# Three graph layers' neighbour mixes as quarter-array products, with tighter buffers and eight groups under way

## The chip, the cores and the metric

The kernel runs on one core of one Trainium2 chip, with the other cores idle. The metric is the time of the program on the device in microseconds (us), from its first to its last instruction; lower is better. All data are float32. The engines that appear below are TensorE (PE in the profile: matrix products, with its weight loads as PEld), VectorE (DVE), ScalarE (ACT), GpSimd (POOL) and the DMA queue that SyncE (SP) issues to. TensorE writes its results to PSUM, which this kernel uses as eight banks of 128 partitions by 512 float32 columns; the other engines copy them from there to SBUF.

## The reference, cut to what matters

The input is 128 graphs of 64 nodes with 256 features each; all graphs share one 64 x 64 adjacency matrix. Four residual layers follow one another:

```python
h = maximum(layernorm(x), 0); x = x + L0(h, adj, ...)   # two adjacency mixes, then four small LSTMs
h = maximum(layernorm(x), 0); x = x + L1(h, adj, ...)   # Laplacian mix, attention with 4 heads, MLP
h = maximum(layernorm(x), 0); x = x + L2(h, adj, ...)   # graph attention
h = maximum(layernorm(x), 0); x = x + L3(h, adj, ...)   # mixes with eigenvectors U of the Laplacian

# what the change touches:
# L1:  xp  = einsum('mn,bnf->bmf', L_norm, h)           # 64 x 64 mix of the nodes of each graph
# L2:  h_prime = einsum('bij,bjo->bio', attention, Wh)  # a mix of its own for each graph
# L3:  agg = einsum('mn,bnd->bmd', U.T, h)
#      out = relu(agg @ W1 + b1) @ W2 + b2
#      result = einsum('nm,bmd->bnd', U, out)
```

Each mix multiplies a 64 x 64 matrix with the 64 nodes of one graph.

## The kernel before

A tile of 128 partitions holds two graphs of 64 nodes. `X[g]` holds eight tiles (16 graphs); layer 0 works on these eight groups. Layers 1 to 3 work on 16 half groups of `HT = 4` tiles (eight graphs each). Since two graphs lie on the 128 partitions, the 64 x 64 mixing matrices are stored as 128 x 128 block-diagonal matrices: the upper left and the lower right quarter hold the matrix, the other two quarters are zero (`adjTb`, `lapb`, `Ub`, `UTb`, and in layer 2 the transposed attention weights `pT`).

The mixes of layers 1, 2 and 3 go through one helper. For each half of the features (`c`) and each tile (`t`) it multiplies a full 128 x 128 block of the activations (the stationary operand) with the 128 x 128 block-diagonal matrix (the moving operand); the result comes out transposed, features on the partitions:

```python
tok = lambda t: slice(t * P, (t + 1) * P)      # P = 128
bat = lambda b: slice(b * N, (b + 1) * N)      # N = 64

def mix_fm(h, m):
    dst = fm()                                  # a "big" buffer, seen as [128, 2, 512]
    for c in range(2):
        ps = bank("mix")
        for t in range(HT):
            PE.matmul(ps[:, tok(t)], h[:, t, tok(c)], m(t), start=True, stop=True)
        evac(dst[:, c, :], ps, 1)               # ScalarE copy of 128 x 512
    return dst

# layer 1:  lx = mix_fm(h, lambda t: lapb)
# layer 2:  aT = mix_fm(h, lambda t: pT[:, tok(t)])
# layer 3:  aT = mix_fm(h, lambda t: Ub)
# ... and layer 3's second mix, on 128 hidden features:
ps = bank("u")
for t in range(HT):
    PE.matmul(ps[:, tok(t)], hid[:, t, :], UTb, start=True, stop=True)
V.tensor_tensor(uT, ps.rearrange("p (t f) -> p t f", t=HT), vec(C3), op=ALU.add)
```

Layer 1's attention already uses 64 x 64 products, in two runs of 32 products per half group. Each product takes one quarter of the array: which half of the partitions its operands lie on picks the rows, which half of the partitions the result goes to picks the columns.

```python
ps = [bank("qk") for m in range(2)]
half = lambda i: slice(i * N, i * N + N)
with plan.burst():
    for b, m, r in [(b, m, r) for b in range(2 * HT) for m in range(2) for r in range(2)]:
        PE.matmul(ps[m][half(r ^ m), bat(b)], qT[half(r), m, bat(b)], kT[half(r), m, bat(b)], start=True, stop=True)
...                                              # softmax, transposes
po = [bank("o") for i in range(2)]
with plan.burst():
    for m, t, i, r in [(m, t, i, r) for m in range(2) for t in range(HT) for i in range(2) for r in range(2)]:
        PE.matmul(po[i][half(r), bat(m * HT + t)], v[half(i), t, bat(2 * m + r)], pT[half(i), m, bat(2 * t + (r ^ m))], start=True, stop=True)
```

The order of instructions on each engine is not that of the source. All operations are recorded first; then a list scheduler on the host (`Plan`) walks through a cost model and fixes each engine's order, the buffer that each value gets and the bank that each product writes. `plan.burst()` makes a run of products one operation of that plan. The parts that matter here:

```python
def burst(self):
    ...
    self.run.cost = 0.3 + 0.036 * len(self.run.calls)    # us, in the plan's model

def rank(self, op):
    ...                                                  # lower goes first
    g = min(max(op.group, 0), self.ends)
    return (g, 8 * max(op.group - g, 0) - op.path, op.index)

# pools
"big": [C([P, HT * (D + 2)], f"big{i}") for i in range(NBIG)],     # 8 buffers of 1032 columns
...
def more(ap, groups):                  # regions that become "big" buffers once `groups` are done
    n = HT * (D + 2)
    for i in range(ap.shape[1] // n):
        late["big", len(pools["big"])] = groups
        pools["big"].append(ap[:, i * n:(i + 1) * n])

more(arena[:, (NG - NEARLY) * GT * D:], (EIG,))          # 6144 columns
more(whh[3], tuple(range(NG)))                           # 2048 columns
more(mids, tuple(range(NG)))                             # 4096 columns
...                                                      # later: each of six X places, 2048 columns

def window(oldest):                    # how many groups may be under way
    return max(oldest, 0) + 2 - oldest if oldest < NG - 1 else max(oldest, REST) + 6 - oldest
```

So after layer 0 at most six half groups are under way at once. The eigenvectors of layer 3 are computed beside layer 0, mostly on VectorE.

Of the kernel before, what the change touches and what calls it, by code (L numbers as in the profile page):

```python
# [8 lines left out]
ALU = mybir.AluOpType  # L9
# [3 lines left out]
N = 64  # L13
# [53 lines left out]
class Plan:  # L67
# [34 lines left out]
    @contextmanager  # L102
    def burst(self):

        self.run, self.whole = None, True
        yield
        self.run.cost = 0.3 + 0.036 * len(self.run.calls)
        self.run.lat = self.run.cost + 0.22
        self.run, self.whole = None, False

# [206 lines left out]
    def rank(self, op):  # L317
        if op.group == self.aside:
            return (-2 if op.eng == "PE" else 1000, op.index)
        if op.eng == "SP":  # L320
            return (op.group, 0, op.index)
        g = min(max(op.group, 0), self.ends)
        return (g, 8 * max(op.group - g, 0) - op.path, op.index)

    def issue(self):
        real = lambda a: a.real() if isinstance(a, Virt) else a
# [538 lines left out]
P = 128  # L865
D = 256
NT = 64
GT = 8
NG = NT // GT
HT = 4  # L870
# [3 lines left out]
SETUP, WEIGHTS, ATTN, REST, EIG = -1, NG, NG + 1, NG + 2, 1000  # L874
NBIG, NMID, NSTAT, NATTN = 8, 8, 14, 4
# [36 lines left out]
def gnn_kernel(ctx: ExitStack, tc: tile.TileContext, a, out):  # L912
    nc = tc.nc
# [3 lines left out]
    def C(shape, name):  # L917
        return pool.tile(list(shape), F32, name=name)
# [4 lines left out]
    whh = [None] + [C([P, 8 * D], f"Whh{p}") for p in range(1, 4)]  # L923
    mids = C([P, NMID * 512], "mids")
    pools = {
        "big": [C([P, HT * (D + 2)], f"big{i}") for i in range(NBIG)],
        "mid": [mids[:, i * 512:(i + 1) * 512] for i in range(NMID)],
        "stat": [C([P, HT * 10], f"stat{i}") for i in range(NSTAT)],
        "attn": [wih[3][:, i * HT * P:(i + 1) * HT * P] for i in range(NATTN)],
# [3 lines left out]

    def more(ap, groups):

        n = HT * (D + 2)
        for i in range(ap.shape[1] // n):
            late["big", len(pools["big"])] = groups
            pools["big"].append(ap[:, i * n:(i + 1) * n])
# [3 lines left out]
    more(mids, tuple(range(NG)))  # L943

    def window(oldest):
        return max(oldest, 0) + 2 - oldest if oldest < NG - 1 else max(oldest, REST) + 6 - oldest

    def reserve(kind, oldest):
        if oldest < NG:
# [8 lines left out]
    plan = Plan(tc, {"PE": nc.tensor, "V": nc.vector, "ACT": nc.scalar, "G": nc.gpsimd, "SP": nc.sync}, pools, late, reserve, window, EIG, REST + NT // HT - 6, slack)  # L958
    PE, V, ACT, G, SP = (plan.proxy(e) for e in ("PE", "V", "ACT", "G", "SP"))

    def bank(name):
        return plan.value("bank")
# [158 lines left out]
    vec = lambda v, n=HT: v.unsqueeze(1).to_broadcast([P, n, v.shape[-1]])  # L1121
    tok = lambda t: slice(t * P, (t + 1) * P)
    bat = lambda b: slice(b * N, (b + 1) * N)

    def tm(n=HT, f=D):

# [173 lines left out]
    def evac(dst, src, i):  # L1300
        if i % 2:
            ACT.copy(dst, src)
        else:
            V.tensor_copy(dst, src)
# [43 lines left out]
    def mix_fm(h, m):  # L1348

        dst = fm()  # L1350
        for c in range(2):
            ps = bank("mix")
            for t in range(HT):
                PE.matmul(ps[:, tok(t)], h[:, t, tok(c)], m(t), start=True, stop=True)
            evac(dst[:, c, :], ps, 1)
        return dst

    def layer1(x):
        h = relu_norm(x)
        lx = mix_fm(h, lambda t: lapb)  # L1360
        x1 = tm()
        for t0 in (0, 2):
            ps = proj_tm(lambda c, t: lx[:, c, tok(t)], Wc, 2, t0)
            V.tensor_add(x1[:, t0:t0 + 2, :], ps.rearrange("p (t f) -> p t f", t=2), vec(bc, 2))
        norm(x1)
        for t0 in (0, 2):
            xp, hp = x1[:, t0:t0 + 2, :], h[:, t0:t0 + 2, :]
            V.tensor_mul(xp, xp, vec(g1, 2))
            G.tensor_add(xp, xp, vec(be1, 2))
            V.scalar_tensor_tensor(xp, xp, 0.0, hp, op0=ALU.max, op1=ALU.add)  # L1370
        x1T = to_fm(x1)
        qT, kT, v = fm(), fm(), tm()
        for m in range(2):
            evac(qT[:, m, :], proj_fm(Wq, x1T, m), 0)
            evac(kT[:, m, :], proj_fm(Wk, x1T, m), 1)
        for t0 in (0, 2):
            evac(pair(v, t0), proj_tm(lambda c, t: x1T[:, c, tok(t)], Wv, 2, t0), 1)
        for t0 in (0, 2):
            G.tensor_add(x1[:, t0:t0 + 2, :], x1[:, t0:t0 + 2, :], vec(bo, 2))


        ps = [bank("qk") for m in range(2)]
        half = lambda i: slice(i * N, i * N + N)
        with plan.burst():
            for b, m, r in [(b, m, r) for b in range(2 * HT) for m in range(2) for r in range(2)]:
                PE.matmul(ps[m][half(r ^ m), bat(b)], qT[half(r), m, bat(b)], kT[half(r), m, bat(b)], start=True, stop=True)
        s = tm(4 * HT, N)
        for m in range(2):
            sm = s[:, m * 2 * HT:(m + 1) * 2 * HT, :]
            V.scalar_tensor_tensor(sm, ps[m].rearrange("p (b k) -> p b k", k=N), 0.125, vec(mask1, 2 * HT), op0=ALU.mult, op1=ALU.add)  # L1390
            stat = plan.value("stat")
            softmax_shift(sm, stat[:, :2 * HT])
            ACT.activation(sm, sm, AF.Exp)
            ssum = stat[:, 2 * HT:4 * HT]
            V.reduce_sum(ssum, sm, axis=AX.X)
            V.reciprocal(ssum, ssum)
            G.tensor_mul(sm, sm, ssum.unsqueeze(2).to_broadcast([P, 2 * HT, N]))

        pT = fm()
        for m in range(2):  # L1400
            evac(pT[:, m, :], transposes([flat(s[:, (m * HT + t) * 2:(m * HT + t) * 2 + 2, :]) for t in range(HT)]), m)
        oT = fm()
# [5 lines that stand above are left out]
        for i in range(2):  # L1408
            evac(oT.rearrange("p c (t b n) -> p c t b n", t=HT, b=2)[:, :, :, i, :], po[i].rearrange("p (c t n) -> p c t n", c=2, t=HT), i)
        x2 = tm()  # L1410
        for t0 in (0, 2):
            ps = proj_tm(lambda c, t: oT[:, c, tok(t)], Wo, 2, t0)
            V.tensor_add(x2[:, t0:t0 + 2, :], ps.rearrange("p (t f) -> p t f", t=2), x1[:, t0:t0 + 2, :])
        norm(x2)
        x2T = fm()
        for c in range(2):
            ACT.activation(x2T[:, c, :], transposes([x2[:, t, tok(c)] for t in range(HT)]), AF.Identity, scale=g2c[:, c:c + 1], bias=be2c[:, c:c + 1])
        V.tensor_mul(x2, x2, vec(g2))
        for t0 in (0, 2):
            G.tensor_add(x2[:, t0:t0 + 2, :], x2[:, t0:t0 + 2, :], vec(b2, 2))  # L1420
        mT = [fm() for i in range(2)]
        for m in range(4):
            ACT.activation(mT[m // 2][:, m % 2, :], proj_fm(W1, x2T, m), AF.Gelu, bias=b1[:, m:m + 1])
        for t0 in (0, 2):
            ps = proj_tm(lambda c, t: mT[c // 2][:, c % 2, tok(t)], W2, 4, t0)
            V.tensor_add(pair(x2, t0), ps, pair(x2, t0))
        for t0 in (0, 2):
            G.tensor_add(x[:, t0:t0 + 2, :], x[:, t0:t0 + 2, :], vec(be3, 2))
        norm(x2)
        for t0 in (0, 2):  # L1430
            V.tensor_mul(x2[:, t0:t0 + 2, :], x2[:, t0:t0 + 2, :], vec(g3, 2))
            V.tensor_add(x[:, t0:t0 + 2, :], x[:, t0:t0 + 2, :], x2[:, t0:t0 + 2, :])

    def layer2(x):
# [16 lines left out]
        V.tensor_max(e, e, e2)  # L1451
        softmax_shift(e, stat[:, :HT])
        attn = plan.value("attn").rearrange("p (t k) -> p t k", t=HT)
        for half in range(2):
            r = slice(half * N, half * N + N)
            ACT.activation(attn[r, :, r], e[r], AF.Exp)
        ssum = stat[:, HT:2 * HT]
        V.reduce_sum(ssum, attn, axis=AX.X)
# [9 lines left out]
    def layer3(x):  # L1468
        h = relu_norm(x)
        for t0 in (0, 2):  # L1470
            G.tensor_add(x[:, t0:t0 + 2, :], x[:, t0:t0 + 2, :], vec(b3b, 2))
        aT = mix_fm(h, lambda t: Ub)
        hid = tm(HT, P)
        ps = bank("hid")
        for t in range(HT):
            for c in range(2):
                PE.matmul(ps[:, tok(t)], aT[:, c, tok(t)], W3a[:, c, :], start=c == 0, stop=c == 1)
        V.tensor_tensor(hid, ps.rearrange("p (t f) -> p t f", t=HT), vec(nb3a), op=ALU.max)
        uT = tm(HT, P)
        ps = bank("u")  # L1480
        for t in range(HT):
            PE.matmul(ps[:, tok(t)], hid[:, t, :], UTb, start=True, stop=True)
        V.tensor_tensor(uT, ps.rearrange("p (t f) -> p t f", t=HT), vec(C3), op=ALU.add)
        for t0 in (0, 2):
            ps = proj_tm(lambda c, t: uT[:, t, :], W3b.unsqueeze(1), 1, t0)
            V.tensor_add(pair(x, t0), ps, pair(x, t0))
# [68 lines left out]
```

## Time and profile before

| | |
|---|---|
| time, median of 3 runs | 2274.92 us (2273.73 to 2276.86) |
| span of the profiled run | 2274.8 us |
| instructions | 33,569 |
| TensorE products (records) | 11,316, busy 2244.4 us |
| VectorE | busy 1685.7 us |
| ScalarE | busy 977.3 us |
| GpSimd | busy 564.0 us |
| last product with `adjTb` (layer 0's mixes) starts at | 1282.9 us |
| first product with `lapb` (layer 1's mix) starts at | 1272.7 us |
| first product with `Ub` (layer 3's mix) starts at | 1547.1 us |

A page of the profile has the busy time of each engine, the span in 40 slices with the busy share of each engine in tenths, and the chain of work that ended last. An engine's group of instructions is named by operation, the result's tile, the operands' tiles, and the shape. Since every instruction passes through the scheduler, all have the same source line (L331), and groups are told apart by tiles and shapes. Each float32 product appears as two records of TensorE (and two weight loads). A record's shape has the moving operand's columns: `128*128 128x256` uses the full array with 256 columns, `64*64 64x64` a quarter with 64 columns. A record's duration includes the way through the array, which overlaps the next record; the interval from one start to the next is what a product costs. "Busy" counts the overlapped stretch once.

### The profile page before, as it was taken

The numbers are of one execution on the slowest core, as the hardware profiler recorded it, in microseconds if no ns is written. First come the engines' busy times: TensorE is split into PE (matmuls) and PEld (weight loads), VectorE is DVE, ScalarE is ACT, GpSimd is POOL, SyncE is SP. The second block draws the span as 40 slices with busy tenths as digits, with TensorE's granted clock in tenths as the row PEclk, the third lists the DMA queues.
The fourth block names the chain that finished last, engine by engine and source line by source line (L and its number), as shares of the span: only waits on it lengthen the run. The fifth ranks groups of instructions, "written<-read, shape, count | busy, mean of one in ns | idle before, by whom it ended". The sixth has DMA issues, their size and how long they took to land.

```text
span 2274.8 us, 33569 instructions
## 1 busy us (share of the span) xinstructions
PE 2244.4 (99%) x11316; PEld 1585.8 (70%) x11316; DVE 1685.7 (74%) x6942; ACT 977.3 (43%) x1915; POOL 564.0 (25%) x856
## 2 busy tenths in 40 slices
PE   9999999999999999999999999999999999999997
PEld 6578468468558558558558658767777677776786
DVE  6656666656799999999988823667678868867775
ACT  3333333333323323323433343455555546555763
POOL 3001100200100100100100203454544655555342
PEclk9999999999999999999999999999999999999999
DMA  7000000000000000000000011000000000000001
GB/s 250 0 1 19 1 1 25 32 1 1 1 1 1 1 1 1 1 1 1 5 1 1 7 38 32 1 1 10 11 20 10 10 29 11 29 10 1 2 18 39
DMA packets 27660, 35.48 MB, mean 16 GB/s; under 512 B 3552, under 2 KB 24928, under 8 KB 26976
## 3 DMA queue, kind: packets, MB, share of 16 engines
q1 hardware_dynamic: 26384, 32.29, 4.2%
q8 instruction: 89, 1.46, 0.3%
q10 hardware_dynamic: 1104, 1.05, 0.2%
q14 instruction: 83, 0.68, 0.1%
HBM read 22.85 MB, written 10.49 MB: 15 GB/s over the span
## 4 chain that ended last, share of the span: by engine, by line
PE 91%; DVE 5%; ACT 2%; POOL 1%; issue 1%; DMA 0%; SPq 0%; DVEq 0%; ACTq 0%
PE bank L331 91%; DVE arena L331 1%; DVE stat L331 1%; DVE big L331 1%; DVE x L331 1%; POOL stat L331 1%; ACT arena L331 1%; DVE mids L331 0%; ACT mids L331 0%; ACT big L331 0%; DMA adj<-in_adj_dram 0%; ACT x L331 0%; ACT Wih L331 0%; DVE Whh L331 0%; POOL x L331 0%
## 5 line engine op out<-in xcount | busy, mean ns | idle before, releaser
L331 PE MATMUL bank<-big,Wih 128*128 128x256 f32 (+2 forms) x2592 | 865.1, 476 | 0.9 <-DVE arena L331 0.3
L331 PEld LDWEIGHTS bank<-big,Wih 128*128 128x128 f32 x2592 | 481.6, 190 | 268.4 <-issue 165.9
L331 ACT ACTIVATE mids<-bank,bl 128x256 f32<-128x256 f32 (+2 forms) x624 | 344.2, 562 | 628.6 <-PE bank L331 617.7
L331 PE MATMUL bank<-big,Whh 128*128 128x256 f32 (+3 forms) x1704 | 538.0, 450 | 0.0
L331 PEld LDWEIGHTS bank<-big,Whh 128*128 128x128 f32 x1704 | 319.3, 191 | 140.3 <-issue 74.6
L331 DVE TENSOR_TENSOR arena<-arena 64x21 f32<-64x21 f32 (+6 forms) x2314 | 374.9, 193 | 34.1 <-POOL arena L331 1.0
L331 POOL TENSOR_SCALAR stat<-stat 128x4 f32<-128x4 f32 (+1 forms) x228 | 66.2, 291 | 726.6 <-DVE stat L331 713.0
L331 DVE TENSOR_TENSOR big<-big,mids 128x256 f32<-128x256 f32 (+2 forms) x192 | 93.7, 488 | 163.5 <-ACT mids L331 162.1
L331 DVE TENSOR_TENSOR big<-mids 128x512 f32<-128x512 f32 (+2 forms) x256 | 145.9, 574 | 37.6 <-ACT mids L331 33.7
L331 ACT ACTIVATE mids<-big 128x256 f32<-128x256 f32 (+2 forms) x176 | 89.8, 510 | 103.5 <-DVE big L331 66.8
L331 DVE TENSOR_SCALAR arena<-arena 64x1 f32<-64x1 f32 (+5 forms) x596 | 117.1, 204 | 8.4
L331 POOL TENSOR_TENSOR stat<-stat,mhalf 128x4 f32<-128x4 f32 (+1 forms) x114 | 119.3, 1049 | 6.8
L331 POOL TENSOR_TENSOR arena<-arena 64x1 f32<-64x1 f32 x66 | 41.9, 635 | 311.5 <-DVE arena L331 165.3
L331 PE MATMUL bank<-Wih,big 128*128 128x256 f32 (+1 forms) x520 | 117.6, 362 | 1.2 <-ACT big L331 1.2
L331 PEld LDWEIGHTS bank<-Wih,big 128*128 128x128 f32 x520 | 90.9, 190 | 20.2 <-issue 8.6
L331 ACT COPY big<-bank 128x512 f32<-128x512 f32 x107 | 59.2, 583 | 80.6 <-PE bank L331 65.4
L331 PEld LDWEIGHTS bank<-adjTb,mids 128*128 128x128 f32 x512 | 70.8, 196 | 26.7 <-issue 17.5
L331 ACT ACTIVATE mids<-x,stat 128x256 f32<-128x256 f32 x92 | 48.6, 592 | 89.7 <-POOL stat L331 89.1
L331 DVE SCALAR_TENSOR_TENSOR arena<-arena 64x1 f32<-64x1 f32 (+4 forms) x389 | 77.2, 205 | 10.5 <-POOL arena L331 4.1
L331 POOL MEMSET arena<- 64x2 f32 (+5 forms) x72 | 8.0, 113 | 309.2 <-DVE arena L331 309.1
L331 DVE BATCH_NORM_STATS2 stat<-x 128x6 f32<-128x256 f32 x228 | 83.4, 409 | 0.0
L331 PE MATMUL bank<-adjTb,mids 128*128 128x128 f32 x512 | 73.6, 282 | 3.0 <-ACT mids L331 2.9
(342 smaller groups left out, 3388.6 us busy)
## 6 DMA issues: line engine op xcount, KB each, us to landing
x<-in_x_dram SPq DMA_DIRECT2D x7, 1024.0 KB, 13.7
out_dram<-x SPq DMA_DIRECT2D x24, 256.0 KB, 2.3
Wih<-in_WihT_dram SPq DMA_DIRECT2D x3, 1024.0 KB, 16.6
Whh<-in_WhhT_dram SPq DMA_DIRECT2D x3, 1024.0 KB, 12.3
put<-x SPq DMA_DIRECT2D x2, 1024.0 KB, 4.6
arena<-put SPq DMA_DIRECT2D x2, 1024.0 KB, 5.0
out_dram<-arena SPq DMA_DIRECT2D x8, 256.0 KB, 2.2
Whh<-in_W_dram SPq DMA_DIRECT2D x2, 512.0 KB, 3.7
```

The source lines that it names most:

```text
L331: getattr(self.engines[op.eng], name)(*map(real, args), **{k: real(a) for k, a in kw.items()})
```

## The change

The mixes of layers 1 to 3 become runs of 64 x 64 products that leave the zero quarters out. A new helper `mix` makes them: per tile and half of the features four products, one for each quarter of the array, where `i` is the graph of the tile and `r` the half of the features. Results of graph `i` go to bank `ps[i]`, so each run writes two banks, and the copies then put the columns of the two graphs back into alternating places of 64. The second mix of layer 3 runs in the same way with 16 products, and its addition of `C3` becomes two of half size. Layer 0's mixes stay as they were.

Beside this, the buffers shrink from 1032 to 1024 columns, so that the regions that are cut into buffers give more of them; the window goes from six to eight half groups; the plan's model of a run's cost goes from 0.3 + 0.036 n to 0.1 + 0.034 n us; and the weight by which later groups stand back goes from 8 to 6.

```diff
-        self.run.cost = 0.3 + 0.036 * len(self.run.calls)
+        self.run.cost = 0.1 + 0.034 * len(self.run.calls)
...
-        return (g, 8 * max(op.group - g, 0) - op.path, op.index)
+        return (g, 6 * max(op.group - g, 0) - op.path, op.index)
...
-        "big": [C([P, HT * (D + 2)], f"big{i}") for i in range(NBIG)],
+        "big": [C([P, HT * D], f"big{i}") for i in range(NBIG)],
...
-        n = HT * (D + 2)
+        n = HT * D
...
-        return ... else max(oldest, REST) + 6 - oldest
+        return ... else max(oldest, REST) + 8 - oldest
...
+    def mix(src, m, nt, nc=2):
+        ps = [bank("mix") for i in range(2)]
+        with plan.burst():
+            for c in range(nc):
+                for t in range(nt):
+                    for i, r in ((0, 0), (0, 1), (1, 0), (1, 1)):
+                        PE.matmul(ps[i][half(r), bat(c * nt + t)], src(t, c)[half(i), half(r)], m(t)[half(i), half(i)], start=True, stop=True)
+        return [p[:, :nc * nt * N].rearrange("p (c t n) -> p c t n", c=nc, t=nt) for p in ps]
...
     def mix_fm(h, m):
         dst = fm()
-        for c in range(2):
-            ps = bank("mix")
-            for t in range(HT):
-                PE.matmul(ps[:, tok(t)], h[:, t, tok(c)], m(t), start=True, stop=True)
-            evac(dst[:, c, :], ps, 1)
+        for i, ps in enumerate(mix(lambda t, c: h[:, t, tok(c)], m, HT)):
+            evac(dst.rearrange("p c (t b n) -> p c t b n", t=HT, b=2)[:, :, :, i, :], ps, 1)
         return dst
...
         uT = tm(HT, P)
-        ps = bank("u")
-        for t in range(HT):
-            PE.matmul(ps[:, tok(t)], hid[:, t, :], UTb, start=True, stop=True)
-        V.tensor_tensor(uT, ps.rearrange("p (t f) -> p t f", t=HT), vec(C3), op=ALU.add)
+        for i, ps in enumerate(mix(lambda t, c: hid[:, t, :], lambda t: UTb, HT, 1)):
+            V.tensor_tensor(uT.rearrange("p t (b n) -> p t b n", b=2)[:, :, i, :], ps[:, 0], vec(C3[:, half(i)]), op=ALU.add)
```

More of the change, by code (lines that the diff above doesn't have):

```diff
@@ L945, in window @@
     def window(oldest):
-        return max(oldest, 0) + 2 - oldest if oldest < NG - 1 else max(oldest, REST) + 6 - oldest
+        return max(oldest, 0) + 2 - oldest if oldest < NG - 1 else max(oldest, REST) + 8 - oldest
     def reserve(kind, oldest):
@@ L1123, in gnn_kernel @@
     bat = lambda b: slice(b * N, (b + 1) * N)
+    half = lambda i: slice(i * N, i * N + N)
+    def mix(src, m, nt, nc=2):
[6 more added lines that the diff above has]
+        return [p[:, :nc * nt * N].rearrange("p (c t n) -> p c t n", c=nc, t=nt) for p in ps]
     def tm(n=HT, f=D):
@@ L1382, in layer1 @@
         ps = [bank("qk") for m in range(2)]
-        half = lambda i: slice(i * N, i * N + N)
         with plan.burst():
@@ L1453, in layer2 @@
         attn = plan.value("attn").rearrange("p (t k) -> p t k", t=HT)
-        for half in range(2):
-            r = slice(half * N, half * N + N)
+        for i in range(2):
+            r = half(i)
             ACT.activation(attn[r, :, r], e[r], AF.Exp)
```

## The prediction

> **What bounds the kernel now.** I read the page's first two parts and its chain first, to find the engine that sets the end.
>
> ```profile
> span 2274.8 us, 33569 instructions
> PE 2244.4 (99%) x11316; PEld 1585.8 (70%) x11316; DVE 1685.7 (74%) x6942; ACT 977.3 (43%) x1915; POOL 564.0 (25%) x856
> ...
> PE   9999999999999999999999999999999999999997
> ...
> DVE  6656666656799999999988823667678868867775
> ...
> PE 91%; DVE 5%; ACT 2%; POOL 1%; issue 1%; DMA 0%; SPq 0%; DVEq 0%; ACTq 0%
> ```
>
> TensorE is busy in every slice, and 91% of the chain is its own work. VectorE is full only in slices 12 to 21 (some 650 to 1250 us), where it computes eigenvectors beside layer 0. Layers 1 to 3 run from about 1270 us, and there VectorE has a quarter to spare. So a product removed from TensorE in that stage should come out of the time, unless a wait takes its place. How much waiting there is already, the busy times by stretch show (columns: stretch, its length, then busy us and instructions of PE, PEld, DVE, ACT, POOL, the clock, the DMA share and GB/s):
>
> ```profile
> 1500.00:1700.00 200.00, 196.95 (x1408) 150.28 (x1411) 144.00 (x415) 114.97 (x198) 100.27 (x137) 1.00 0.03 9
> 1700.00:1900.00 200.00, 195.03 (x1370) 146.44 (x1362) 150.94 (x408) 109.39 (x193) 99.45 (x134) 1.00 0.05 17
> 1900.00:2100.00 200.00, 198.92 (x1526) 147.94 (x1526) 150.81 (x406) 111.01 (x194) 112.61 (x146) 1.00 0.04 14
> 2100.00:2200.00 100.00, 100.00 (x653) 75.96 (x652) 75.22 (x229) 72.19 (x115) 42.52 (x63) 1.00 0.02 6
> 2200.00:2275.00 75.00, 60.01 (x358) 53.78 (x356) 45.01 (x140) 27.05 (x52) 23.29 (x38) 0.93 0.11 36
> ```
>
> TensorE is idle 3.1 + 5.0 + 1.1 + 0 = 9 us from 1500 to 2200, and 15 us in the last 75, where the groups run out. Short waits hide in "busy", because a record's duration includes its way through the array. Taking each record's start minus the one before, less the usual interval of its shape, I get 20 us of waiting from 1500 to 2200, 18 us after, and 51 us in the whole run.
>
> What a product costs is read from the timeline of TensorE alone (start, duration, group; "x" counts records, two to a product):
>
> ```profile
> 1713.23 3.19 PE L331 MATMUL bank<-Wih,arena 128*128 128x256 f32 x14
> 1716.34 1.16 PE L331 MATMUL bank<-arena,big 64*64 64x64 f32 x64
> 1717.44 0.70 PE L331 MATMUL bank<-mids,same 128*128 128x256 f32 x2
> 1717.97 1.01 PE L331 MATMUL bank<-ident,arena 128*128 128x128 f32 x6
> ...
> 1737.25 4.05 PE L331 MATMUL bank<-Whh,x 128*128 128x256 f32 x18
> 1741.14 0.60 PE L331 MATMUL bank<-ident,big 128*128 128x128 f32 x4
> ...
> 1750.10 1.95 PE L331 MATMUL bank<-lapb,big 128*128 128x128 f32 x16
> 1751.88 1.89 PE L331 MATMUL bank<-Wih,mids 128*128 128x256 f32 x8
> ```
>
> The last two lines are one old mix: 16 records, 1751.88 - 1750.10 = **1.78 us**, so 0.111 us a record and 0.222 a product. The first four lines are a run of 32 quarter products, as the attention of layer 1 already has: 1717.44 - 1716.34 = 1.10 us inside. But its neighbours pay as well. A 256-column record takes (1741.14 - 1737.25) / 18 = 0.216 us. The 14 ahead of the run took 3.11 us instead of 3.02: 0.09 more to get in. The two behind it took 0.53 instead of 0.43: 0.10 more to get out. So a run costs 1.10 + 0.09 + 0.10 = **1.29 us**. I looked at all 32 runs of the trace: those that stand alone have 0.94 us from the first to the last record, 0.15 from there to the next product, about 0.1 ahead and 0.1 behind. Within a run, four records start nearly together, then comes the next four 0.059 us later.
>
> **What the Trainium skill says.** "TensorEngine Tiling (Array Packing)", section Tiling Modes, Key Properties, says that tiles of the array work independently, and that changing the tiling mode drains TensorE. The trace agrees with both: 32 products in 1.10 us instead of 32 x 0.11, and about 0.19 us for getting in and out. The same page, Gotcha 1: PSUM Pressure, says that different row tiles write to different PSUM banks and may not share one at once. That is why the new helper needs two banks even for the 16-product mix, which fills half of each; no run before shows what sharing would do. Its section PSUM Bottleneck says that after tiling the copies out of PSUM may become the bound; here ScalarE and VectorE have 45% and 25% to spare in this stage, so I don't expect it.
>
> **The change part by part.**
>
> (1) Three mixes per half group: each removes 8 products and adds a run of 32. 1.78 - 1.29 = 0.49 us saved. There are 16 half groups, so 48 x 0.49 = **23.5 us**.
>
> (2) Layer 3's second mix: 4 products, 4 x 0.222 = 0.89 us, become a run of 16. Eight rounds of four records fewer take 8 x 0.059 = 0.47 us off the run of 1.29, which leaves 0.82. Saved 0.07 us, 16 x 0.07 = **1 us**. The fixed cost of the mode eats this one.
>
> (3) Runs that happen to lie next to each other pay the way in and out once. The trace has one such pair (128 records at 1483 us). With four more runs per half group there will be some more; I allow 1 us.
>
> (4) ScalarE's copies: still two per mix, but with places of 64 columns. Layer 1's attention has such copies: 0.585 us with places of 64 and 0.585 us without, at the median. Nothing added. VectorE gets 16 additions more: one of 128 x 512 at 0.69 us becomes two of 128 x 256. The 128 x 256 additions between SBUF tiles take 0.41 us, so I estimate 2 x 0.41 - 0.69 = 0.13 us, 2 us in all, in a stage where VectorE has a quarter idle. On the path: nothing.
>
> (5) Latency: before, the first bank of a mix could be copied after 4 products (0.9 us), while the other was filled. Now both banks are done at the end of the run (1.1 us), and the copies stand one behind the other: some 0.3 us more from the mix to the next projection, three times per half group. With eight half groups under way this is covered, except at the end, where it adds about 1 us.
>
> (6) Buffers and window: 1024 columns divide the regions without rest. The arena's 6144 columns give 6 instead of 5, one weight region 2 instead of 1, `mids` 4 instead of 3. With the 8 of their own that is 20 instead of 17 after layer 0, and each of the six places of X gives 2 instead of 1 when it comes free. Six groups had 2.8 each, eight have 2.5, then more. So eight groups can be fed, and when one waits on VectorE or GpSimd another has a product ready. The plan's cost of a run falls from 0.3 + 0.036 x 32 = 1.45 us to 1.19, nearer to the 1.29 measured, so planned and real order fit better. I estimate that the 20 us of waits from 1500 to 2200 fall by some 12, and the 18 us at the end by 2 (a weight of 6 instead of 8 lets the last groups finish closer together), less the 1 us of (5). Together **13 us**. This is a judgement, the other terms are arithmetic.
>
> (7) Layer 0 has none of these mixes, and TensorE waits 6 us in it after 50 us: nothing to gain.
>
> Sum: 23.5 + 1 + 1 + 13 = 38.5 us; 2274.9 - 38.5 = **2236 us**, 1.7% less.
>
> **The rivals.** (A) The products saved turn into waits. If the helpers (VectorE, 75% busy; two banks held by each run; GpSimd's slow steps) set the pace, TensorE idles more and only a few us of 25 remain: about 2262 us. For it: the waits above end on VectorE and ScalarE, and the plan's order is fixed ahead, so a late operation stops all behind it. Against it: no helper is over 76% in any stretch, and 100 us went by at 2100 without idle time. (B) The schedule gain is larger: eight groups remove nearly all waits, 20 us in the middle and half of the 18 at the end, which gives 2274.9 - 25.5 - 29 = 2220 us. For it: from 1310 to 1500 the waits measured from starts are under 1 us, so a near waitless order exists. Against it: the end is a chain of the last groups, which a wider window doesn't shorten. (C) The new order of quarters (both column halves of one row half in turn) works worse than the old. If two instead of four ran together, a run would take some 0.9 us more and the time would be about 2285 us. Against it: attention's second run has this same order, and all runs show 0.94 us. I hold it unlikely.
>
> **Range and chances.** Parts (1) to (3) I hold good to 5 us. The waits can change between 10 us more and 30 less. That gives 2222 to 2254 us for 8 in 10. Two per cent less is 2229.4 us, which needs 20 us out of the waits: chance 0.24. Slower by over 2% would need (C) and worse: 0.02. The rest, 0.74, is within 2%.
>
> **What would show it.** In the changed profile: 48 x 48 + 16 x 24 = 2688 more TensorE records (11,316 to about 14,000); the 64 x 64 runs still 1.10 us each with 64 records, 0.6 us with 32; no full-array product on `lapb`, `Ub` or `UTb` after their set-up; TensorE busy near 2220 us; ScalarE's copies still 0.585 us; idle TensorE under 5 us from 1500 to 2150. It is wrong if a run takes over 1.2 us inside, if waits on PSUM copies grow, or if layer 0's end, 1283 us for its last mix, moves by more than 5 us.

## The result and the profile after

The changed kernel takes 2239.20 us, the median of four runs (2237.00 to 2240.61), against 2275.27 us for the kernel before: a ratio of 0.984 with an interval of 0.982 to 0.986, so 36 us less. The prediction said 2236 us, in a range of 2222 to 2254.

The changed kernel's page, the same lines as before:

```profile
span 2236.0 us, 38989 instructions
PE 2206.2 (99%) x14004; PEld 1532.4 (69%) x14004; DVE 1688.3 (76%) x6958; ACT 966.9 (43%) x1911; POOL 559.0 (25%) x856
...
PE   9999999999999999999999999999999999999998
...
DVE  7666666745799999999998943468798777776697
...
PE 88%; DVE 7%; POOL 2%; ACT 1%; issue 1%; DMA 0%; SPq 0%; DVEq 0%; ACTq 0%; POOLq 0%
```

TensorE has exactly the 2688 more records that part (1) and part (2) add up to, it is busy for 38 us less (2206 us, where the prediction's signs named "near 2220"), and it still sets the end. Its share of the chain fell from 91% to 88%, VectorE's rose from 5% to 7%.

Busy times by stretch of the changed kernel (stretch, length, then PE, PEld, DVE, ACT, POOL, clock, DMA share, GB/s):

```profile
1500.00:1700.00 200.00, 195.30 (x2006) 141.31 (x2008) 167.73 (x447) 116.97 (x208) 114.10 (x152) 1.00 0.03 9
1700.00:1900.00 200.00, 198.27 (x2266) 145.15 (x2262) 150.79 (x437) 116.60 (x208) 103.84 (x146) 1.00 0.07 23
1900.00:2100.00 200.00, 199.63 (x2042) 143.34 (x2034) 142.90 (x376) 106.57 (x186) 94.23 (x125) 1.00 0.03 10
2100.00:2200.00 100.00, 97.11 (x1027) 73.48 (x1026) 88.71 (x298) 68.85 (x118) 47.27 (x74) 1.00 0.02 7
2200.00:2236.00 36.00, 28.20 (x499) 23.49 (x497) 21.26 (x55) 11.76 (x23) 12.37 (x17) 0.97 0.22 75
```

From 1500 to 2200 us TensorE is idle 4.7 + 1.7 + 0.4 + 2.9 = 9.7 us: no less than before. But the part after 2200 us, where the groups run out, went from 75 us with 15 idle to 36 us with 8 idle.

The timeline of TensorE alone shows the new runs (start, duration, group; x counts records):

```profile
1713.37 1.16 PE L331 MATMUL bank<-Ub,arena 64*64 64x64 f32 x64
1714.46 1.13 PE L331 MATMUL bank<-Wih,big 128*128 128x256 f32 x4
1715.52 1.16 PE L331 MATMUL bank<-big,Whh 64*64 64x64 f32 x64
1716.61 2.48 PE L331 MATMUL bank<-Wih,big 128*128 128x256 f32 x18
...
1720.70 0.70 PE L331 MATMUL bank<-UTb,mids 64*64 64x64 f32 x32
1721.33 0.33 PE L331 MATMUL bank<-ident,big 128*128 128x128 f32 x1
```

A run of 32 products takes 1714.46 - 1713.37 = 1.09 us from its start to the next product, one of 16 takes 0.63. The four records of 256 columns between two runs take 1.06 us instead of 4 x 0.216 = 0.86: 0.1 behind the first run and 0.1 ahead of the second. All as the attention's runs were before.

### Work and waits

To compare the runs below, I split TensorE's time in each trace. The usual interval of each record's shape is work; the intervals in a run, and the way in and out of it, are work of the run; what a start comes later than that is wait. A record that runs slower under a lower clock adds to the waits too. Before 1310 us (layer 0 and set-up) the waits by this count are 29 to 31 us in all kernels but two: some 3 us less in plan_only and 4 us more in layer0_runs. "Middle" is 1310 to 2150 us, "end" what comes after. All values are us. The first two lines come from the measurement of the change; each other run was timed beside the kernel before, which took 2276.0 to 2276.1 us there, and its ratio is to that. Work and waits are from the profiled run of each kernel and depend by some 3 us on how late starts inside a run are booked (more in no_run).

| kernel | time | ratio (interval) | TensorE's work | waits, middle | waits, end |
|---|---|---|---|---|---|
| before | 2275.3 | 1 | 2203.0 | 18.8 | 18.0 |
| changed | 2239.2 | 0.984 (0.982 to 0.986) | 2173.6 | 17.9 | 8.6 |
| products_only | 2272.1 | 0.9985 (0.9978 to 0.9991) | 2173.2 | 38.9 | 22.3 |
| plan_only | 2257.1 | 0.992 (0.991 to 0.994) | 2203.3 | 11.4 | 8.5 |
| weight8 | 2251.7 | 0.990 (0.988 to 0.991) | 2173.6 | 22.5 | 19.8 |
| window6 | 2241.7 | 0.986 (0.984 to 0.987) | 2171.8 | 22.0 | 11.0 |
| buf1032 | 2237.8 | 0.984 (0.982 to 0.985) | 2173.2 | 17.9 | 8.7 |
| oldcost | 2241.2 | 0.985 (0.984 to 0.986) | 2172.9 | 17.1 | 11.9 |
| u_full | 2248.0 | 0.988 (0.986 to 0.989) | 2175.7 | 21.5 | 12.9 |
| no_run | 2337.6 | 1.026 (1.023 to 1.028) | 2218.2 | 52.9 | 31.3 |
| products_newcost | 2255.6 | 0.991 (0.990 to 0.993) | 2174.0 | 23.4 | 21.9 |
| products_weight6 | 2264.8 | 0.996 (0.995 to 0.997) | 2173.2 | 40.7 | 13.1 |
| products_window8 | 2294.2 | 1.008 (1.007 to 1.009) | 2172.9 | 60.1 | 23.8 |
| layer0_runs | 2234.8 | 0.982 (0.981 to 0.984) | 2162.0 | 19.8 | 9.7 |

### The profile page after: what moved, and what is told of

The parts are those of the page before. It is cut to its first block, busy times and chain, and to the rows that moved or that the text cites. A ratio compares the mean times of both kernels' runs of the same rounds, so it can differ in the third digit from the quotient of the medians.

```text
span 2236.0 us, 38989 instructions
## 1 busy us (share of the span) xinstructions
PE 2206.2 (99%) x14004; PEld 1532.4 (69%) x14004; DVE 1688.3 (76%) x6958; ACT 966.9 (43%) x1911; POOL 559.0 (25%) x856
## 4 chain that ended last, share of the span: by engine, by line
PE 88%; DVE 7%; POOL 2%; ACT 1%; issue 1%; DMA 0%; SPq 0%; DVEq 0%; ACTq 0%; POOLq 0%
PE bank L331 88%; DVE arena L331 2%; DVE big L331 2%; DVE stat L331 2%; POOL stat L331 1%; DVE x L331 1%; DVE mids L331 1%; ACT mids L331 1%; ACT big L331 0%; ACT arena L331 0%; DVE Whh L331 0%; POOL x L331 0%; POOL big L331 0%; DMA adj<-in_adj_dram 0%; ACT x L331 0%
## 5 line engine op out<-in xcount | busy, mean ns | idle before, releaser
L331 PE MATMUL bank<-big,Wih 128*128 128x512 f32 (+2 forms) x2656 | 897.6, 479 | 3.8 <-POOL big L331 1.7
L331 PEld LDWEIGHTS bank<-big,Wih 128*128 128x128 f32 x2656 | 492.9, 190 | 279.7 <-issue 171.1
L331 PE MATMUL bank<-big,Whh 128*128 128x256 f32 (+3 forms) x1768 | 515.3, 431 | 2.1 <-DVE big L331 2.1
L331 PEld LDWEIGHTS bank<-big,Whh 128*128 128x128 f32 (+1 forms) x1768 | 309.4, 186 | 137.5 <-issue 68.3
L331 PE MATMUL bank<-Wih,big 128*128 128x256 f32 (+1 forms) x416 | 94.6, 366 | 0.1
L331 PE MATMUL bank<-Whh,big 128*128 128x256 f32 (+1 forms) x400 | 85.9, 358 | 1.9 <-ACT big L331 1.2
L331 ACT COPY mids<-bank 128x512 f32<-128x512 f32 x100 | 55.2, 586 | 66.3 <-PE bank L331 62.1
L331 PEld LDWEIGHTS bank<-Wih,big 128*128 128x128 f32 x416 | 72.2, 191 | 11.7 <-issue 2.2
L331 PEld LDWEIGHTS bank<-Whh,big 128*128 128x128 f32 (+1 forms) x400 | 62.2, 181 | 22.9 <-issue 10.2
```

The source lines that it names most:

```text
L331: getattr(self.engines[op.eng], name)(*map(real, args), **{k: real(a) for k, a in kw.items()})
```

## The experiments

My theory after the result: 29 us of the 36 are TensorE's work, which comes out of the time one for one because TensorE sets the end, and the plan's parts add some 10 us. Rival A: without the new plan the helpers take the saving back. Rival B: the products do it all.

### The two halves alone

products_only is the changed kernel with the plan's four parts undone:

```diff
-        self.run.cost = 0.1 + 0.034 * len(self.run.calls)
+        self.run.cost = 0.3 + 0.036 * len(self.run.calls)
-        return (g, 6 * max(op.group - g, 0) - op.path, op.index)
+        return (g, 8 * max(op.group - g, 0) - op.path, op.index)
-        n = HT * D                                  # and the pool's own buffers
+        n = HT * (D + 2)
-        ... max(oldest, REST) + 8 - oldest
+        ... max(oldest, REST) + 6 - oldest
```

> The mixes of layers 1 to 3 as runs of quarter products, everything else as before (window of six, buffers of 1032 columns, old weight, old cost of a run in the plan). My theory: the products alone take about 28 us of TensorE work out (100 us of full-array products go, 71 us of runs come), and the waits stay near those of before: about 2247 us. Rival A (the helpers or PSUM banks take it back without the new plan): over 2262 us. Rival B (the products do it all, the plan's parts do nothing): about 2239 us.

Measured: 2272.1 us, 4 us less than before (2276.1 us in the same measurement). TensorE's work fell by 30 us as expected, and nearly all of it came back as waits: 20 more in the middle, 4 more at the end. My theory falls, and the time is the one that rival A named; its reason, helpers or PSUM banks, is another matter. The busy times of this kernel in the two stretches, and those of the kernel before:

```profile
1500.00:2150.00 650.00, 627.74 (x6527) 451.83 (x6526) 497.36 (x1381) 373.39 (x650) 337.41 (x455) 1.00 0.04 13
2150.00:2270.00 120.00, 101.04 (x1276) 79.74 (x1274) 81.58 (x249) 59.37 (x102) 45.00 (x67) 0.94 0.08 28
```

```profile
1500.00:2150.00 650.00, 640.90 (x4686) 481.53 (x4686) 483.01 (x1337) 371.03 (x641) 332.00 (x449) 1.00 0.04 13
2150.00:2275.00 125.00, 110.01 (x614) 92.87 (x611) 82.97 (x259) 63.58 (x110) 46.14 (x68) 0.96 0.08 26
```

TensorE stands idle 22 of 650 us where it was 9, though no helper is over 77% busy (VectorE 497 of 650). So it isn't that an engine became the bound: single results come too late for the order in which TensorE wants them. The profile's list of idle gaps from 1310 us on has 47 of them with 38 us in all, the longest 3.7 us (before: 21 with 18 us). By the tiles' names 31 of the 38 us ended with an instruction that wrote an operand of the waiting product, and only 5 us with one that read a bank, so waits for free PSUM banks are a small part.

plan_only is the other half, the kernel before with the four lines above as in the changed kernel.

> The other half alone: 1024 columns, window of eight, weight 6, new cost of a run, but the mixes as full-array products. My theory: TensorE's work is that of before, only waits can go; with the 10 us fewer that the changed kernel shows, about 2265 us. Rival B: no change, 2275 us. Were the plan the main cause: about 2245 us.

Measured: 2257.1 us, 19 us less than before in the same measurement, twice what the theory gave, with work as before and 17 us fewer waits from 1310 us on. Its two stretches:

```profile
1500.00:2150.00 650.00, 645.21 (x4720) 487.15 (x4720) 481.47 (x1333) 366.92 (x635) 322.85 (x438) 1.00 0.04 13
2150.00:2255.00 105.00, 96.40 (x576) 81.75 (x574) 80.54 (x251) 57.36 (x104) 44.00 (x67) 0.99 0.09 31
```

Alone, the halves give 4 and 19 us; together 36. They are not independent: the products, which take some 30 us of work out each time, are worth 4 us under the old plan and 18 us under the new one (2257.1 to 2239.2). Even there most of the rest comes back as waits: 11.4 us in the middle become 17.9.

### Which part of the plan, from the side of the changed kernel

Each of these undoes one line in the changed kernel: the weight (8), the window (6), the buffers (1032 columns), the cost of a run (0.3 + 0.036 n).

> The changed kernel with the old weight of 8 for later groups. If the weight of 6 is what lets the last groups finish closer together (waits after 2150 us: 18 before, 9 after), this costs some 7 us: 2246 us, and the waits at the end come back. If the window does it, 2239 us.

Measured: 2251.7 us, 12.5 more. The waits at the end go from 8.6 to 19.8 us. This is the largest of the four.

> The changed kernel with six half groups under way instead of eight. If the two more groups are what keeps TensorE fed, as I predicted for 1500 to 2200 us, waits there grow from 12 to 20 us or more and the time is about 2248 us. If the weight or the buffers do it, 2239 us.

Measured: 2241.7 us, 2.5 more. Waits grow by 4 in the middle and 2 at the end, while work is 2 less because runs lie next to each other more often. The window is worth much less than I gave it, and 2.5 us isn't clear of noise: the two intervals overlap.

> The changed kernel with buffers of 1032 columns: 17 instead of 20 after layer 0, for the same eight half groups. My theory (buffers feed the eight groups): waits from 1310 to 2150 us grow by 5 us or more, about 2246 us. Rival (buffers were never short): 2239 us.

Measured: 2237.8 us, no difference. Seventeen buffers feed eight half groups as well as twenty: in the changed kernel nothing shows that buffers were short.

> The changed kernel with the old cost of a run in the plan's model (1.45 us for 32 products instead of 1.19; 1.29 measured with its way in and out). My theory: the plan is off by 0.16 us a run either way, so little changes: 2236 to 2243 us. Rival (a truer cost makes the order fit): 2246 us or more.

Measured: 2241.2 us. Within the expected range; under the new weight and window the other cost is worth some 2 us, which isn't clear of noise (the intervals overlap).

The end of weight8, and that of the changed kernel:

```profile
1500.00:2150.00 650.00, 641.78 (x6727) 464.81 (x6726) 503.24 (x1395) 378.91 (x660) 339.05 (x457) 1.00 0.04 13
2150.00:2251.00 101.00, 83.94 (x1091) 67.53 (x1089) 70.47 (x218) 51.07 (x89) 34.68 (x56) 0.93 0.10 33
```

```profile
1500.00:2150.00 650.00, 643.20 (x6675) 466.17 (x6674) 502.27 (x1392) 376.33 (x661) 331.79 (x455) 1.00 0.04 13
2150.00:2236.00 86.00, 75.31 (x1133) 60.60 (x1131) 69.12 (x220) 44.42 (x83) 40.03 (x57) 0.99 0.12 39
```

Up to 2150 us the two are nearly alike (8.2 and 6.8 us idle; with the waits inside "busy" weight8 has 4.6 us more). After it weight8 has 101 us left with 17 idle, the changed kernel 86 with 11. The starts of layer 3's second mix tell how the last six half groups end: at 2160 to 2244 us with a weight of 8 (84 us apart), at 2176 to 2228 us with 6 (51 us), at 2178 to 2267 us in the kernel before (89 us). It is the weight that goes with this in the other kernels too: 51 to 58 us apart with a weight of 6 (68 in no_run), 84 to 86 with 8 (products_only, products_newcost, products_window8). With the smaller weight the last groups finish closer together, and TensorE waits less at the end.

### Which part, from the side of the products alone

The three that could matter, one at a time, added to products_only.

> Quarter products with everything of before but the new cost of a run. The products alone gained 4 us, though TensorE had 29 us less work: 25 us went into new waits. Theory C (the plan thought each of 81 runs 0.16 us longer than it is, so its order was made for a slower TensorE): the waits go back to about 66 us and the time is about 2250 us. Theory W (window of six and weight of 8 starve TensorE of ready products, whatever the plan's cost): about 2270 us.

Measured: 2255.6 us, 16 less than products_only; the waits in the middle go from 38.9 to 23.4 us, those at the end stay. Its two stretches:

```profile
1500.00:2150.00 650.00, 638.83 (x6689) 460.38 (x6682) 493.77 (x1397) 382.25 (x663) 342.10 (x466) 1.00 0.04 13
2150.00:2254.00 104.00, 85.98 (x1094) 69.25 (x1092) 71.25 (x221) 51.66 (x89) 34.93 (x57) 0.92 0.10 32
```

The time is nearer to theory C's 2250 us than to W's 2270: the cost of a run in the plan does change the waits. That it does so because it is nearer to the truth isn't shown. Both values miss the measured 1.29 us, the old one by 0.16 and the new one by 0.10; no other value was run; and any new value gives a new order, which can gain or lose some us by itself (the 8 us of waits in u_full, below).

> Quarter products with everything of before but the weight of 6. In the changed kernel the old weight alone cost 12.5 us, 11 of them in waits after 2150 us. If that gain is there without the other parts, about 2260 us, with the 22 us of waits at the end down to some 11; if it needs the window or the new cost, about 2270 us.

Measured: 2264.8 us, 7 less. The waits at the end go from 22.3 to 13.1 us, those in the middle stay. So the weight works on the end in both surroundings (9 and 11 us).

> Quarter products with everything of before but the window of eight. In the changed kernel the old window cost only 2.5 us. Theory W: here, with the other parts old, eight groups take some 10 to 15 us of the 34 us of waits from 1500 to 2150 us away: about 2260 us. Theory C: about 2270 us.

Measured: 2294.2 us, 22 us more than products_only and slower than the kernel before. Both theories missed. Two more groups under way gain little, if anything, in the changed kernel and do harm here. Busy times from 1500 to 1700 us:

```profile
1500.00:1700.00 200.00, 175.09 (x1802) 126.77 (x1802) 138.11 (x367) 96.49 (x173) 95.42 (x127) 0.93 0.02 7
```

TensorE idles for 25 of 200 us, and no other engine is over 70% busy. Its waits from 1310 us on (who waited for whom, us in total, times, the longest):

```profile
PE bank L331 <- ACT Wih L331: 17.3, 4, 5.1
PE bank L331 <- DVE big L331: 13.2, 10, 5.2
PE bank L331 <- ACT arena L331: 4.8, 5, 1.6
```

A few long waits make most of it: four on ScalarE's exponentials of layer 2 (`Wih` holds the attention tiles then), ten on VectorE. A fixed order of instructions has TensorE stand before a product that isn't ready; presumably other groups had products ready behind it, which the profile doesn't tell. A long wait also costs more than itself. The clock that the first line shows is 0.93, against 1.00 in the changed kernel, and after the longest waits the records are slower for some us:

```profile
1667.31 1.12 PE L331 MATMUL bank<-ident,Wih 128*128 128x128 f32 x4 [4.89 <-ACT Wih L331]
1668.22 5.19 PE L331 MATMUL bank<-mids,Whh 128*128 128x512 f32 x8
```

Record by record, the first three intervals of these eight records of 512 columns are 0.85 us instead of 0.43. Weight8 has the window of eight and the weight of 8 too, but the new cost (and 1024 columns), and takes 2251.7 us, 42 us less. Why the old cost is that bad with eight and 8, and nearly harmless with eight and 6, isn't settled by these runs.

### How the runs are made

no_run takes `with plan.burst()` away from the helper, so that the plan places each quarter product by itself.

```diff
-        with plan.burst():
+        if True:
```

> The changed kernel with each quarter product an operation of its own in the plan, so that quarter and full-array products alternate: the compiled order has 202 runs of quarter products on TensorE instead of 82. My theory (each way in and out of a run costs 0.09 ahead, 0.11 in the last interval and 0.10 behind, 0.30 us): 120 x 0.30 = 36 us more, about 2275 us, nearly all of the gain. Rival (the switch is hidden when other products are ready): 2239 to 2245 us.

Measured: 2337.6 us, 98 more than the changed kernel and slower than before. The trace has 215 runs, where 202 were expected. The 133 more ways in and out are 45 us of work by the count, 2218.2 against 2173.6, at 0.33 us each, about as expected; the other half, which neither theory foresaw, is waits, 84 against 26 us in middle and end. Those may come from the plan, which takes 0.08 us for a lone quarter product where the trace has 0.03; that wasn't separated.

u_full puts layer 3's second mix back to four full-array products.

```diff
-        for i, ps in enumerate(mix(lambda t, c: hid[:, t, :], lambda t: UTb, HT, 1)):
-            V.tensor_tensor(uT...[:, :, i, :], ps[:, 0], vec(C3[:, half(i)]), op=ALU.add)
+        ps = bank("u")
+        for t in range(HT):
+            PE.matmul(ps[:, tok(t)], hid[:, t, :], UTb, start=True, stop=True)
+        V.tensor_tensor(uT, ps.rearrange("p (t f) -> p t f", t=HT), vec(C3), op=ALU.add)
```

> The changed kernel with layer 3's second mix as four full-array products per half group again. My prediction gave this part 1 us. The compiled order has 69 runs instead of 82, so 13 of the 16 short runs stand alone: quarter work 16 x 0.47 + 13 x 0.30 = 11.4 us against 16 x 0.89 = 14.3 us. So 3 us more, 2242 us; within 2 us of the changed kernel if the predicted 1 us is right. If the short runs cost more than they save: under 2237 us.

Measured: 2248.0 us, 9 more. The work is 2 us more, near the 3 of the direct count; 8 us are waits, in an order that is new once more. So the 9 us say little about what the short runs themselves are worth.

layer0_runs goes further: layer 0's mixes too become runs, of 16 products.

```diff
-            for c in range(2):
-                for t in range(2):
-                    PE.matmul(ahp[...], h[:, t, tok(c)], adjTb, start=True, stop=True)
-            ACT.copy(ah, ahp)
+            for i, ps in enumerate(mix(lambda t, c: h[:, t, tok(c)], lambda t: adjTb, 2)):
+                ACT.copy(ah.rearrange("p (c t b n) -> p c t b n", c=2, t=2, b=2)[:, :, :, i, :], ps)
# the second mix, with y, in the same way; its two additions of C0T go by graph instead of by half
```

> The changed kernel with layer 0's mixes as quarter runs too, 16 products each. The compiled order has 126 runs instead of 82. TensorE: 256 full-array products go, 256 x 0.224 = 57 us; 1024 quarter products come, 1024 x 0.0295 = 30 us, with 44 more ways in and out at 0.30 = 13 us. So 14 us less, 2226 us, if the work of TensorE is what counts. If layer 0 loses it to longer copies (ScalarE copies twice 128 x 256 instead of once 128 x 512), 2235 to 2245 us.

Measured: 2234.8 us. TensorE's work falls by 11.6 us, close to the 14 expected, and some 7 of them come back as waits (4 of these before 1310 us). Its stretch of layer 0, and that of the changed kernel:

```profile
50.00:1310.00 1260.00, 1253.10 (x6156) 819.08 (x6154) 1005.13 (x4997) 446.66 (x1004) 116.52 (x233) 1.00 0.02 5
```

```profile
50.00:1310.00 1260.00, 1255.95 (x4839) 838.41 (x4838) 998.61 (x4986) 448.26 (x982) 113.69 (x232) 1.00 0.01 5
```

It has the lowest median of all, but its interval (0.981 to 0.984) overlaps that of the changed kernel (0.982 to 0.986): its 4 us aren't clear of noise.

## Why the prediction was right, and where it was not

**Parts (1) to (3), TensorE's work.** Predicted 25.5 us less, measured 29.4: the full-array work fell by 100.3 us and the runs rose from 41.2 to 112.1. Runs and mixes cost what the trace of before showed (1.09 us inside, 0.1 ahead, 0.1 behind). The term that was mis-sized is part (3): of 96 runs, 14 lie next to another, which leaves 82, where before one of 32 did. Thirteen at 0.30 us are 4 us, against the 1 us allowed. The prediction's 0.19 us for the way in and out counts the neighbours alone; the run's own last interval is 0.11 us longer than those between fours and sits in its 1.10 us, which makes 0.30 in all.

**Part (2), the short runs.** Predicted 1 us. The work that u_full has more is 2 us; its other 8 us are waits.

**Parts (4) and (5).** ScalarE's copies with places of 64 columns take 0.586 us, the others 0.585. The 32 half-size additions take 0.414 us each, so 0.14 us more for each pair, and VectorE's busy time grew by 2.6 us (2 predicted). Layer 0's last mix starts at 1270.5 us, 1.3 earlier. (It was 1271.8 us before: the 1282.9 us of the table before, and the 1283 and 1483 us of the prediction, are read on the trace's own clock, which is 11 us ahead of the span that all other times count from.)

**Part (6), waits: the sum was near, the step was wrong.** Predicted 13 us fewer, 12 of them in the middle through buffers and the window, 1 at the end. Measured from 1310 us on: 10.3 fewer, 0.9 in the middle and 9.4 at the end. The end is the weight, which I had given 2 us. In the changed kernel the buffers did nothing and the window 2.5 us, within noise. The sign that I named for it, TensorE idle for under 5 us from 1500 to 2150, failed as well: it was 6.8 (9.1 before). That the sum of the waits came out near is luck: one place gained 11 us less than I said, the other 8 us more.

**What the sum hid.** I added work saved and waits saved as if each stood alone, and took the work saved to come out of the time by itself because TensorE is 99% busy. products_only shows that under the old plan it doesn't: rival A, which I held for about 2262 us, would have been nearer for the products alone (2272). Under the new plan the products are worth 18 us, still not the 25.5 of the sum, and the plan alone brings 19, not 13. The new cost of a run, which in part (6) was half a sentence, saves 16 us when it is added to the products alone. The forecast met the time because the change brought both together; the same steps would have missed products_only by more than 20 us. Rival B's 2220 us asked for nearly all waits to go, and 26 us of them stayed. Rival C can be ruled out: the new order of quarters runs as fast as the old.

## What to carry to other kernels

When one engine is busy all the time and its order is fixed ahead by a plan, removing its work shortens the time only as far as the others' results are there earlier as well: count work and waits apart, and after a change of durations try the planner with the new ones. Undo the tuning that comes with a change and measure the change alone, since 30 us of work turned out to be worth 4 us under one plan and 18 under another. A gain of some us from one constant of such a plan need not carry over: the window of eight was worth 2.5 us, within noise, in one setting and cost 22 in another. A run of quarter-array products pays only if it is long enough for its way in and out (0.3 us here), so they should be packed and laid next to each other.

## What the runs showed of the hardware

Going from full-array to quarter products and back costs TensorE about 0.3 us in all, with the same medians in the traces of all fourteen kernels: the record ahead of a run takes 0.09 us longer, the last interval of the run is 0.15 us where those between fours are 0.04, and the record behind it takes 0.10 us more. The kernel with 215 runs (no_run) has the same three values as those with 31 to 126. ScalarE's and VectorE's copies out of PSUM took the same time whether they wrote 512 columns in a row or places of 64 (0.585 and 0.586 us on ScalarE; all of VectorE's between 0.65 and 0.69). After a wait of 4.9 us TensorE's records of 512 columns took 0.85 us instead of 0.43 for a few us.
